# Second layer of a mixture of graph experts: an odd slot tile in a place of its own, pairs nested behind it, another order of the products, and a GpSimd drain after each expert

## The chip, the cores and the metric

The kernel runs on one core of a Trainium2 chip. The metric is the device time of one execution in microseconds. Before the change it is 805.65 us (median of 3 runs, 804.23 to 806.14).

## The reference, cut to what matters

A graph of 1250 nodes with rows of 512 features goes through a pre-norm attention layer and then through a mixture of four graph experts, of which each node keeps the two with the largest gates. Only the second part is touched:

```python
def sage_conv(h, W_l, b_l, W_r):
    aggr = segment_sum(h[src], dst) * inv_deg       # mean over the neighbours
    return aggr @ W_l + b_l + h @ W_r
...
gates = softmax(x @ gate_W + gate_b)
top_v, top_i = top_k(gates, 2)
...
for e in range(4):
    h = x
    for l in range(2):
        h = relu(sage_conv(h, Wl[e, l], bl[e, l], Wr[e, l]))
    # weighted by the gate where expert e is one of the node's two, and added to the output
```

The first layer of an expert is needed on all nodes, since the second averages over neighbours. The second is needed only on the nodes that chose the expert: 54, 917, 1049 and 480 nodes for experts 0 to 3 with these inputs.

## The kernel before, in words

**Layer 1.** For each expert, `layer1(t)` computes two tiles of 125 nodes at once. The 2x2 block product (own features and neighbour mean against Wr and Wl, each in column halves) is done with seven products P1 to P7 (four steps of a 128x256 fp32 matmul each, eight matmuls in the trace) where eight would be needed; sums of operands and results are VectorE's. The result is written to DRAM (`h1`, for gathering) and kept on chip as a high and a low half (`split`, L115 to L121: ScalarE writes h_hi, VectorE h_lo).

**Slots.** `number_slots` (L666) and `fill_slots` (L712) number the nodes of each expert: slot tile i (a "place") holds 128 of the chosen nodes, and `reads`, `writes` and `gate` hold for each slot the node's row and gate. An expert has NS = 10 places. The counts of nodes go into `many`, from which each engine loads them into a register.

**Layer 2.** For a place, GpSimd gathers with an indirect DMA the packed counts of its nodes' neighbours (`fetch_counts`, L787, tile asel, a ring of four), which `unpack` (L790) turns into a matrix AS: transposes on TensorE, digits on VectorE (L802), five casts and the copy of one column `inv` (L808) on ScalarE. It gathers the nodes' own rows of h1 (`fetch_own`, L813, tile hsel, a ring of two). `sums_of` multiplies AS with h_hi and h_lo of all ten node tiles (20 matmuls of 512 columns, p_s), `mean_of` scales with inv and transposes, `features` transposes the own rows with a ReLU. `pair_of_slots` (L944) then makes two places with the seven products, in the order P1, P7, P2, P4, P5, P6, P3; P1 and P7 lie in the halves of one PSUM bank. `one_of_slots` (L977) makes a single place with four products. `put` (L932) applies ReLU and gate on ScalarE (L935) and adds the tile into the output with an accumulating indirect DMA (L936); tile y is a ring of two.

**Control flow.** `second_layer` (L995) is a nest that calls itself: at place i, if the expert has more than (i+1) x 128 nodes the pair i, i+1 is made, and then, if there are more than (i+2) x 128 (L1011), the nest goes on at i+2; otherwise (the Else arm) place i is made alone. So a single place stands at the end of an expert. The outermost If (here `counts[e] > 0`) stands in the expert loop, L1017 to L1038.

**Order.** The tile scheduler orders the instructions of each engine within a block of the program; across the Ifs the order is that of the blocks. The first `layer1` call of the next expert is issued ahead of the Ifs of the current one, and its other calls, with the counts of its first four places, behind them. GpSimd issues all 82 indirect DMAs of a run in one queue. At the end `total` is loaded into a register and compared with the number of edges (L1374 to L1376); the branch jumps over a general version of the kernel that isn't needed here.

Of the kernel before, what the change touches and what calls it, by code (L numbers as in the profile page):

```python
# [42 lines left out]
def tile_sorted_graph(  # L43
# [92 lines left out]
        return t  # L136

    SLOTS = 128
    NS = -(-N // SLOTS)
    packs = dram.tile([N, SC + 1], F32, name="packs")  # L140


# [10 lines left out]
    sums = const.tile([T, ND * len(chunks)], F32, name="sums")  # L153
    ones_h = const.tile([128, 128], BF16, name="ones_h")
    nc.vector.memset(ones_h, 1.0)
    many = const.tile([1, NE], I32, name="many")
    AT = adj.tile([T, NT, N], F32R, name="AT")
    AT32 = AT.bitcast(F32)

# [492 lines left out]
    def bias_rows(e):  # L652
# [3 lines left out]

    first_bias = bias_rows(0)

    spots = xall[:, 3:8, :].rearrange("p a n -> p (a n)").bitcast(BF16).rearrange(
        "p (c n) -> p c n", n=SLOTS)  # L660
    tells = xall[:, 8:, :].rearrange("p a n -> p (a n)").bitcast(BF16)[:, :NE * NT * FLD * NS].rearrange(
        "p (c f q) -> p c f q", f=FLD, q=NS)

    book = ctx.enter_context(tc.tile_pool(name="book", bufs=1, side="right"))

    def number_slots():  # L666

        flat = chosen.rearrange("p e t -> p (e t)")  # L670
        p = bank("p_n")
        nc.tensor.matmul(p[:T, :NE * NT], before, flat, start=True, stop=True)
        nc.tensor.matmul(p[:T, NE * NT:2 * NE * NT], ones_h[:T, :T], flat, start=True, stop=True)
        pv = p[:T, :2 * NE * NT].rearrange("p (a e t) -> p a e t", a=2, e=NE)
        off = book.tile([T, NE, NT + 1], F32, name="off")
        nc.vector.memset(off[:, :, 0], 0.0)
        for t in range(NT):
            nc.vector.tensor_add(off[:, :, t + 1], off[:, :, t], pv[:, 1, :, t])
        nc.vector.tensor_copy(many, off[:1, :, NT])
        at = book.tile([T, NE, NT], F32, name="at")  # L680
        nc.vector.tensor_add(at, pv[:, 0], off[:, :, :NT])
        at = at.rearrange("p e t -> p (e t)")
        qt = book.tile([T, NE * NT], F32, name="qt")
        nc.vector.tensor_scalar(qt, at, 1.0 / SLOTS, -(0.5 - 0.25 / SLOTS), op0=OP.mult, op1=OP.add)
        nc.vector.tensor_scalar(qt, qt, ROUND, -ROUND, op0=OP.add, op1=OP.add)
        nc.vector.scalar_tensor_tensor(at, qt, float(-SLOTS), at, op0=OP.mult, op1=OP.add)

        nc.vector.scalar_tensor_tensor(qt, qt, 1.0, flat, op0=OP.add, op1=OP.mult)
        left = book.tile([T, NE, NT], F32, name="left")
        nc.vector.tensor_copy(left, g.rearrange("p t e -> p e t"))  # L690
        left = left.rearrange("p e t -> p (e t)")
        for f in range(2, FLD):
            nc.vector.tensor_copy(told[:, :, f], left)
            if f + 1 < FLD:
                nc.vector.tensor_sub(left, left, told[:, :, f])
        for e in range(NE):
            c = slice(e * NT, (e + 1) * NT)
            nc.vector.tensor_tensor(spots[:, c, :], steps_h[:, None, :].to_broadcast([T, NT, SLOTS]),
                                    at[:, c, None].to_broadcast([T, NT, SLOTS]), op=OP.is_equal)

        mine = mix_tiles[0][0].rearrange("p k n -> p (k n)").bitcast(BF16)[:T, :NE * NT * NS].rearrange(
            "p (c q) -> p c q", q=NS)
        nc.vector.tensor_tensor(mine, steps_h[:, None, 1:NS + 1].to_broadcast([T, NE * NT, NS]),
                                qt[:, :, None].to_broadcast([T, NE * NT, NS]), op=OP.is_equal)
        nc.vector.tensor_tensor(tells, mine[:, :, None, :].to_broadcast([T, NE * NT, FLD, NS]),
                                told[:, :, :, None].to_broadcast([T, NE * NT, FLD, NS]), op=OP.mult)
# [31 lines left out]
    while mean_whole:  # L738
        if len(mean_whole) == 1:
# [6 lines left out]
            first_mix = mix_weights(w0)  # L746
            mix_nodes(0)
        next_mean()
    counts = [nc.values_load(many[:1, e:e + 1], min_val=0, max_val=N,
                             skip_runtime_bounds_check_because="it is compared, and addresses nothing")  # L750
              for e in range(NE)]
    halves.release()
    node.release()
    adj.release()
# [172 lines left out]
    def mean_of(p, iv):  # L927
        agg = aggs()
        nc.vector.tensor_scalar(agg, p, iv, None, op0=OP.mult)  # L929
        return features(agg, gTs, AF.Copy)  # L930
# [8 lines left out]
    def halves_of(*names):  # L939
        for name in names:  # L940
            p = bank(name)
            yield from (p[:, h * HD:(h + 1) * HD] for h in range(2))

    def pair_of_slots(second, r, g, spare_sums, e, i):  # L944

        B11, B21, B22, T1, T2, T3, T4, bl1, br1 = second
        (A11, A21), (A12, A22) = r, g
        S1, S2, S3, S4 = (t.rearrange("p (k n) -> p k n", k=KF) for t in spare_sums)
        P1, P7, P2, P4, P5, P6 = halves_of("p_y", "p_y", "p_y")
        P3 = bank("p_y")[:, :HD]  # L950
        ya, yb = ys(), ys()
        C11, C12, C21, C22 = ya[:, :HD], ya[:, HD:], yb[:, :HD], yb[:, HD:]
        nc.vector.tensor_sub(S3, A11, A21)
        times(P1, (A11, B11))
        nc.vector.tensor_add(C11, P1, bl1)
        nc.vector.tensor_add(S1, A21, A22)
        times(P7, (S3, T3))
        nc.vector.tensor_sub(S2, S1, A11)
        nc.vector.tensor_add(C22, C11, P7)
        times(P2, (A12, B21))  # L960
        nc.vector.tensor_sub(S4, A12, S2)
        times(P4, (A22, T4))
        times(P5, (S1, T1))
        nc.vector.tensor_add(C12, P5, br1)
        times(P6, (S2, T2))
        nc.vector.tensor_add(C21, C22, P6)
        nc.vector.tensor_add(C22, C21, C12)
        nc.vector.tensor_add(C21, C21, P4)  # L968
        put(yb, e, i + 1)
        nc.vector.tensor_add(C12, C12, C11)  # L970
        nc.vector.tensor_add(C12, C12, P6)
        nc.vector.tensor_add(C11, C11, P2)
        times(P3, (S4, B22))
        nc.vector.tensor_add(C12, C12, P3)
        put(ya, e, i)

    def one_of_slots(second, r, p, iv, e, i):  # L977

# [13 lines left out]
        nc.vector.tensor_add(C12, C12, Q)  # L992
        put(y, e, i)

    def second_layer(of, e, i, own, AS, asel):  # L995

        (a, b), ivs, hs, h1 = *zip(*AS), of.hs, of.h1
        with tc.If(counts[e] > (i + 1) * SLOTS) as two:  # L998

            later = [fetch_counts(e * NS + n) for n in range(i + 4, min(i + 6, NS))]  # L1000
            p = [sums_of(a, hs), sums_of(b, hs)]
            g = [mean_of(p[0], ivs[0])]
            r = [features(v, rTs, AF.Relu) for v in own]
            if i + 2 < NS:
                own = [fetch_own(e * NS + n, h1) for n in (i + 2, i + 3)]
            if asel:
                AS = [unpack(v) for v in asel]
            g.append(mean_of(p[1], ivs[1]))
            pair_of_slots(of.second, r, g, of.spare_sums, e, i)
            if i + 2 < NS:  # L1010
                with tc.If(counts[e] > (i + 2) * SLOTS):  # L1011
                    second_layer(of, e, i + 2, own, AS, later)
        with two.Else():
            one_of_slots(of.second, own[0], sums_of(a, hs), ivs[0], e, i)

    ahead = [w0]
    now = Expert(0)  # L1017
    for e in range(NE):
        now.loads()
        for t in range(min(e, 1), NT // 2):  # L1020
            now.layer1(t)
            if t == NT // 2 - (2 if e == 0 else 3):
                asel = [fetch_counts(e * NS + i) for i in range(4)]
            if t == NT // 2 - (1 if e == 0 else 2):
                AS = [unpack(a) for a in asel[:2]]
        now.finish()
        own = [fetch_own(e * NS + i, now.h1) for i in range(2)]
        of = now
        if e + 1 == NE:
            of.mix_second()  # L1030
        else:
            now = Expert(e + 1)
            now.layer1(0)
            of.mix_second()
        of.spare_sums = [node_sums[(turns[0] + i) % 6] for i in range(2)] + \
            [vs.tiles[(vs.n + i) % 4] for i in range(2)]
        with tc.If(counts[e] > 0):  # L1037
            second_layer(of, e, 0, own, AS, asel[2:])  # L1038


@with_exitstack
# [325 lines left out]
@with_exitstack  # L1367
def tile_gat_then_moe_sage(ctx: ExitStack, tc: tile.TileContext, *args):
    nc = tc.nc
    flag = ctx.enter_context(tc.tile_pool(name="flag", bufs=1))  # L1370
    total = flag.tile([1, 1], I32, name="total")
    tile_sorted_graph(tc, *args, total)
    E = args[1].shape[0]
    counted = nc.values_load(total[:1, :1], min_val=0, max_val=1 << 24,  # L1374
                             skip_runtime_bounds_check_because="it is compared, and addresses nothing")
    with tc.If(counted != E):  # L1376
        tile_any_graph(tc, *args)

# [27 lines left out]
```

## Time and profile before

| | us |
|---|---|
| median of 3 runs | 805.65 (804.23 to 806.14) |
| profiled execution | 806.73 |
| its span | 805.0 |
| TensorE busy | 743.4 |
| VectorE busy | 505.8 |
| ScalarE busy | 265.8 |
| GpSimd busy | 147.4 |
| mean granted TensorE clock | 0.968 |

Layer 1 and layer 2 of the experts take the span from about 249 us to the end. A pair of places takes 24.0 us there, from start to start. The page counts matmuls, vector operations and issued DMAs as busy; branches, register loads and drains are not in its busy times but are in the trace. A timeline row gives start, duration, engine, line, operation, tiles, and in brackets the idle time of the engine before it with what ended it. A wait row gives the total, the number of times and the longest one. The gathers and puts of GpSimd are:

```profile
L813 POOL DMA_INDIRECT hsel<-h,reads x28 | 33.0, 1180 | 227.7 <-issue 94.9
L936 POOL DMA_INDIRECT out_dram<-y,writes x22 | 35.8, 1629 | 195.8 <-ACT y L935 155.6
...
L787 POOL DMA_INDIRECT asel<-packs,reads x32 | 35.4, 1106 | 66.7 <-DVE v L880 56.8
```

The numbers after the bar are the busy time, and the mean of one in ns; a row's DMA lands later than its instruction ends.

### The profile page before, as it was taken

How to read it: one execution, taken by the hardware profiler on the slowest of the kernel's cores; microseconds unless marked ns; L12 is line 12 of the kernel's file. 1: busy time of each engine (PE TensorE's matmuls, PEld its weight loads, DVE VectorE, ACT ScalarE, POOL GpSimd, SP SyncE). 2: the span in 40 equal slices, each digit the busy share in tenths (PEclk: the TensorE clock that was granted, in tenths of full speed). 3: DMA queues.
4: the chain of work that ended last, by engine and by line, in shares of the span. 5: the costliest groups of instructions: out<-in, count | busy, mean ns of one | idle time of the engine just before them, and what ended most of it. 6: DMA issues, size and time to landing. Idle time of an engine off the chain costs nothing. (4 is left out here: it accounts for less than half of the span.)

```text
span 805.0 us, 9845 instructions
## 1 busy us (share of the span) xinstructions
PE 743.4 (92%) x3448; PEld 597.0 (74%) x3448; DVE 505.8 (63%) x1152; ACT 265.8 (33%) x589; POOL 147.4 (18%) x125
## 2 busy tenths in 40 slices
PE   6899999999999999999999997999999997899960
PEld 4677545455998888788888886888888886788850
DVE  7987999599878569267743434678344343466340
ACT  5659766764300012112033322120333230132230
POOL 1000523222002001200313322103133212002220
PEclk9899999999999999999999999999999998999985
DMA  7000001010225412261303323612133224213131
GB/s 189 7 13 7 6 13 58 13 39 1 72 97 159 140 57 74 93 222 43 90 27 66 66 41 94 214 49 83 34 66 62 31 41 109 78 52 86 26 61 15
DMA packets 30331, 54.27 MB, mean 67 GB/s; under 512 B 5786, under 2 KB 8230, under 8 KB 30252
## 3 DMA queue, kind: packets, MB, share of 16 engines
q0 software_dynamic: 6944, 16.58, 10.2%
q1 hardware_dynamic: 15154, 20.80, 8.8%
q10 hardware_dynamic: 8154, 15.91, 5.8%
q8 instruction: 41, 0.67, 0.4%
q14 instruction: 38, 0.31, 0.1%
HBM read 34.10 MB, written 19.82 MB: 67 GB/s over the span
## 5 line engine op out<-in xcount | busy, mean ns | idle before, releaser
L431 PE MATMUL p_o<-hW,P 125*125 125x512 f32 x200 | 93.5, 609 | 2.3 <-DVE P L425 2.3
L923 PE MATMUL p_s<-h_hi,AS 125*128 125x512 f32 x220 | 89.0, 404 | 1.3 <-issue 1.3
L923 PE MATMUL p_s<-h_lo,AS 125*128 125x512 f32 x220 | 86.8, 394 | 0.0
L831 PE MATMUL p<-T,S 128*125 128x256 f32 x320 | 74.8, 386 | 3.1 <-DVE v L880 3.1
L118 ACT ACTIVATE h_hi<-v 125x512 fp32r<-125x512 f32 x40 | 25.2, 630 | 154.7 <-DVE v L895 132.9
L813 POOL DMA_INDIRECT hsel<-h,reads x28 | 33.0, 1180 | 227.7 <-issue 94.9
L936 POOL DMA_INDIRECT out_dram<-y,writes x22 | 35.8, 1629 | 195.8 <-ACT y L935 155.6
L831 PEld LDWEIGHTS p<-T,S 128*125 128x125 f32 x320 | 61.0, 191 | 13.1 <-DVE v L880 3.7
L929 DVE TENSOR_SCALAR agg<-p_s,inv 128x512 f32<-128x512 f32 x22 | 16.5, 751 | 79.8 <-PE p_f L821 43.4
L431 PEld LDWEIGHTS p_o<-hW,P 125*125 125x125 f32 x200 | 36.4, 193 | 39.4 <-issue 34.8
L806 ACT CAST AS<-digs 125x256 fp32r<-125x256 int32 x140 | 51.1, 403 | 19.4 <-DVE digs L802 12.3
L923 PEld LDWEIGHTS p_s<-h_hi,AS 125*128 125x128 f32 x220 | 41.5, 188 | 11.1 <-issue 1.7
L429 POOL TENSOR_TENSOR den<-den,P 125x375 f32<-125x375 f32 (+1 forms) x27 | 38.1, 1412 | 62.6 <-DVE P L425 59.4
L935 ACT ACTIVATE y<-y,gate 128x512 f32<-128x512 f32 x22 | 15.9, 723 | 99.7 <-DVE y L968 71.6
L923 PEld LDWEIGHTS p_s<-h_lo,AS 125*128 125x128 f32 x220 | 41.5, 189 | 9.4
L787 POOL DMA_INDIRECT asel<-packs,reads x32 | 35.4, 1106 | 66.7 <-DVE v L880 56.8
L823 ACT ACTIVATE gT<-p_f 128x512 f32<-128x512 f32 x22 | 13.1, 598 | 97.2 <-PE p_f L821 97.2
L378 DVE TENSOR_SCALAR first<-iota,low,val 125x250 bf16<-125x250 f16 x128 | 45.0, 413 | 0.3 <-PE p_a L382 0.3
L831 PE MATMUL p<-wr,h2T 128*125 128x256 f32 x160 | 39.6, 392 | 4.8 <-DVE S L645 4.1
L328 PE MATMUL p_h<-W_sb,hT 128*125 128x257 f32 x160 | 41.4, 417 | 2.2 <-ACT hT L185 2.1
L553 PE MATMUL p_ag<-AT,h_hi 125*128 125x416 f32 (+1 forms) x120 | 42.4, 355 | 0.0
L553 PE MATMUL p_ag<-AT,h_lo 125*128 125x416 f32 (+1 forms) x120 | 42.1, 352 | 0.0
(222 smaller groups left out, 1515.6 us busy)
## 6 DMA issues: line engine op xcount, KB each, us to landing
h<-v SPq DMA_DIRECT2D x40, 224.0 KB
wl<-in_L_gnn_Wl_dram ACTq DMA_DIRECT2D x7, 1024.0 KB
wr<-in_L_gnn_Wr_dram ACTq DMA_DIRECT2D x7, 1024.0 KB
out_dram<-x SPq DMA_DIRECT2D x10, 224.0 KB
x<-in_x_dram SPq DMA_DIRECT2D x1, 1120.0 KB
packs<-pack SPq DMA_DIRECT2D x10, 109.4 KB
h<-v SPq DMA_DIRECT2D x40, 26.0 KB
W_sb<-in_L_gnn_W_dram SPq DMA_DIRECT2D x4, 256.0 KB
```

Of the source, the lines that this page charges most:

```text
L118: nc.scalar.activation(hi, v, AF.Relu if relu else AF.Copy)
L328: nc.tensor.matmul(p[:T, :HD + 1], hT[:, k, :], W_sb[:, k, half, :], start=(k == 0), stop=(k == KF - 1))
L378: nc.vector.tensor_scalar(hs[:, :SC], iota[:EB, :SC], low[:, j:j + 1], val[:, j:j + 1], op0=OP.is_equal, op1=OP.mult)
L429: nc.gpsimd.tensor_add(den[:, :n], den[:, :n], P[:, :n])
L431: nc.tensor.matmul(po[i][:T, :], P[:, i * T:(i + 1) * T], hW[:, s - 1, :, :HD], start=(s == 1), stop=(s == NT))
L553: nc.tensor.matmul(p[:, :n], h2[s][i][:, m * 128:(m + 1) * 128], AT[:, s, c], start=(s == 0 and i == 0), stop=(s == NT - 1 and i == 1))
L787: nc.gpsimd.indirect_dma_start(a, None, packs, bass.IndirectOffsetOnAxis(reads[:, j:j + 1], 0))
L806: nc.scalar.copy(AS[:, d * SB:(d + 1) * SB, :], dig)
L813: nc.gpsimd.indirect_dma_start(r, None, h1, bass.IndirectOffsetOnAxis(reads[:, j:j + 1], 0))
L831: nc.tensor.matmul(p, A[:, k, :], B[:, k, :], start=(i == 0 and k == 0), stop=(i * KF + k == n - 1))
L923: nc.tensor.matmul(p, A[:, s, :], hs[s][f], start=(s == order[0] and f == 0), stop=(s == order[-1] and f == 1))
L936: nc.gpsimd.indirect_dma_start(out, bass.IndirectOffsetOnAxis(writes[:, j:j + 1], 0), y, None, bounds_check=N - 1, oob_is_err=False, compu ...
```

## The change

- NS becomes 11. Place 0 holds a tile of slots only if the expert's number of tiles is odd; otherwise it stays empty and the tiles lie in places 1 to 10. `number_slots` computes `odd` and shifts the places by it, and `many` gets a second row.
- `second_layer` goes. In the expert loop, `one_of_slots` makes place 0 under `If odds[e] > 0`, and then pairs 1-2, 3-4, 5-6, 7-8 and 9-10 follow in nested Ifs without Else. The counts of places 0 and 1 are unpacked and their own rows fetched ahead of the branches; place 2 is fetched and unpacked inside the first pair's If. So these steps are done for three more places in the run (experts 1 to 3).
- `pair_of_slots` makes P1, P2, P5, P6, P3, puts place i, and then makes P7 and P4 and puts place i+1. P1 and P6, P5 and P7, P2 and P4 share PSUM banks.
- GpSimd gets a `drain` behind each expert's Ifs. In the program as built it stands, for experts 0 to 2, ahead of the next expert's first `fetch_counts`; for expert 3 it stands at the end.
- `total` is loaded in the function that computes it and no longer in the caller; in the program as built, the load still stands behind the last expert.

```diff
@@ -136,7 +136,7 @@
         return t
 
     SLOTS = 128
-    NS = -(-N // SLOTS)
+    NS = -(-N // SLOTS) + 1
     packs = dram.tile([N, SC + 1], F32, name="packs")
 
 
@@ -153,7 +153,7 @@
     sums = const.tile([T, ND * len(chunks)], F32, name="sums")
     ones_h = const.tile([128, 128], BF16, name="ones_h")
     nc.vector.memset(ones_h, 1.0)
-    many = const.tile([1, NE], I32, name="many")
+    many = const.tile([1, 2, NE], I32, name="many")
     AT = adj.tile([T, NT, N], F32R, name="AT")
     AT32 = AT.bitcast(F32)
 
@@ -656,9 +656,9 @@
 
     first_bias = bias_rows(0)
 
-    spots = xall[:, 3:8, :].rearrange("p a n -> p (a n)").bitcast(BF16).rearrange(
+    spots = xall[:, 2:7, :].rearrange("p a n -> p (a n)").bitcast(BF16).rearrange(
         "p (c n) -> p c n", n=SLOTS)
-    tells = xall[:, 8:, :].rearrange("p a n -> p (a n)").bitcast(BF16)[:, :NE * NT * FLD * NS].rearrange(
+    tells = xall[:, 7:, :].rearrange("p a n -> p (a n)").bitcast(BF16)[:, :NE * NT * FLD * NS].rearrange(
         "p (c f q) -> p c f q", f=FLD, q=NS)
 
     book = ctx.enter_context(tc.tile_pool(name="book", bufs=1, side="right"))
@@ -676,7 +676,17 @@
         nc.vector.memset(off[:, :, 0], 0.0)
         for t in range(NT):
             nc.vector.tensor_add(off[:, :, t + 1], off[:, :, t], pv[:, 1, :, t])
-        nc.vector.tensor_copy(many, off[:1, :, NT])
+        nc.vector.tensor_copy(many[:, 0, :], off[:1, :, NT])
+
+        odd = book.tile([T, NE], F32, name="odd")
+        twos = book.tile([T, NE], F32, name="twos")
+        nc.vector.tensor_scalar(odd, off[:, :, NT], 1.0 / SLOTS, 0.5 - 0.25 / SLOTS, op0=OP.mult,
+                                op1=OP.add)
+        nc.vector.tensor_scalar(odd, odd, ROUND, -ROUND, op0=OP.add, op1=OP.add)
+        nc.vector.tensor_scalar(twos, odd, 0.5, -0.25, op0=OP.mult, op1=OP.add)
+        nc.vector.tensor_scalar(twos, twos, ROUND, -ROUND, op0=OP.add, op1=OP.add)
+        nc.vector.scalar_tensor_tensor(odd, twos, -2.0, odd, op0=OP.mult, op1=OP.add)
+        nc.vector.tensor_copy(many[:, 1, :], odd[:1, :])
         at = book.tile([T, NE, NT], F32, name="at")
         nc.vector.tensor_add(at, pv[:, 0], off[:, :, :NT])
         at = at.rearrange("p e t -> p (e t)")
@@ -685,7 +695,10 @@
         nc.vector.tensor_scalar(qt, qt, ROUND, -ROUND, op0=OP.add, op1=OP.add)
         nc.vector.scalar_tensor_tensor(at, qt, float(-SLOTS), at, op0=OP.mult, op1=OP.add)
 
-        nc.vector.scalar_tensor_tensor(qt, qt, 1.0, flat, op0=OP.add, op1=OP.mult)
+        by_expert = qt.rearrange("p (e t) -> p e t", e=NE)
+        nc.vector.tensor_tensor(by_expert, by_expert, odd[:, :, None].to_broadcast([T, NE, NT]),
+                                op=OP.subtract)
+        nc.vector.scalar_tensor_tensor(qt, qt, 2.0, flat, op0=OP.add, op1=OP.mult)
         left = book.tile([T, NE, NT], F32, name="left")
         nc.vector.tensor_copy(left, g.rearrange("p t e -> p e t"))
         left = left.rearrange("p e t -> p (e t)")
@@ -746,9 +759,12 @@
             first_mix = mix_weights(w0)
             mix_nodes(0)
         next_mean()
-    counts = [nc.values_load(many[:1, e:e + 1], min_val=0, max_val=N,
-                             skip_runtime_bounds_check_because="it is compared, and addresses nothing")
-              for e in range(NE)]
+    def loaded(v, most):
+        return nc.values_load(v, min_val=0, max_val=most,
+                              skip_runtime_bounds_check_because="it is compared, and addresses nothing")
+
+    counts, odds = ([loaded(many[:1, i, e:e + 1], N) for e in range(NE)] for i in range(2))
+    all_counted = loaded(total[:1, :1], 1 << 24)
     halves.release()
     node.release()
     adj.release()
@@ -946,33 +962,32 @@
         B11, B21, B22, T1, T2, T3, T4, bl1, br1 = second
         (A11, A21), (A12, A22) = r, g
         S1, S2, S3, S4 = (t.rearrange("p (k n) -> p k n", k=KF) for t in spare_sums)
-        P1, P7, P2, P4, P5, P6 = halves_of("p_y", "p_y", "p_y")
+        P1, P6, P5, P7, P2, P4 = halves_of("p_y", "p_y", "p_y")
         P3 = bank("p_y")[:, :HD]
         ya, yb = ys(), ys()
         C11, C12, C21, C22 = ya[:, :HD], ya[:, HD:], yb[:, :HD], yb[:, HD:]
         nc.vector.tensor_sub(S3, A11, A21)
         times(P1, (A11, B11))
-        nc.vector.tensor_add(C11, P1, bl1)
+        nc.vector.tensor_add(C21, P1, bl1)
         nc.vector.tensor_add(S1, A21, A22)
-        times(P7, (S3, T3))
         nc.vector.tensor_sub(S2, S1, A11)
-        nc.vector.tensor_add(C22, C11, P7)
+        nc.vector.tensor_sub(S4, A12, S2)
         times(P2, (A12, B21))
-        nc.vector.tensor_sub(S4, A12, S2)
-        times(P4, (A22, T4))
+        nc.vector.tensor_add(C11, C21, P2)
         times(P5, (S1, T1))
-        nc.vector.tensor_add(C12, P5, br1)
+        nc.vector.tensor_add(C22, P5, br1)
         times(P6, (S2, T2))
-        nc.vector.tensor_add(C21, C22, P6)
-        nc.vector.tensor_add(C22, C21, C12)
-        nc.vector.tensor_add(C21, C21, P4)
-        put(yb, e, i + 1)
-        nc.vector.tensor_add(C12, C12, C11)
-        nc.vector.tensor_add(C12, C12, P6)
-        nc.vector.tensor_add(C11, C11, P2)
+        nc.vector.tensor_add(C21, C21, P6)
+        nc.vector.tensor_add(C12, C21, C22)
         times(P3, (S4, B22))
         nc.vector.tensor_add(C12, C12, P3)
         put(ya, e, i)
+        times(P7, (S3, T3))
+        nc.vector.tensor_add(C21, C21, P7)
+        nc.vector.tensor_add(C22, C22, C21)
+        times(P4, (A22, T4))
+        nc.vector.tensor_add(C21, C21, P4)
+        put(yb, e, i + 1)
 
     def one_of_slots(second, r, p, iv, e, i):
 
@@ -992,27 +1007,6 @@
         nc.vector.tensor_add(C12, C12, Q)
         put(y, e, i)
 
-    def second_layer(of, e, i, own, AS, asel):
-
-        (a, b), ivs, hs, h1 = *zip(*AS), of.hs, of.h1
-        with tc.If(counts[e] > (i + 1) * SLOTS) as two:
-
-            later = [fetch_counts(e * NS + n) for n in range(i + 4, min(i + 6, NS))]
-            p = [sums_of(a, hs), sums_of(b, hs)]
-            g = [mean_of(p[0], ivs[0])]
-            r = [features(v, rTs, AF.Relu) for v in own]
-            if i + 2 < NS:
-                own = [fetch_own(e * NS + n, h1) for n in (i + 2, i + 3)]
-            if asel:
-                AS = [unpack(v) for v in asel]
-            g.append(mean_of(p[1], ivs[1]))
-            pair_of_slots(of.second, r, g, of.spare_sums, e, i)
-            if i + 2 < NS:
-                with tc.If(counts[e] > (i + 2) * SLOTS):
-                    second_layer(of, e, i + 2, own, AS, later)
-        with two.Else():
-            one_of_slots(of.second, own[0], sums_of(a, hs), ivs[0], e, i)
-
     ahead = [w0]
     now = Expert(0)
     for e in range(NE):
@@ -1022,7 +1016,7 @@
             if t == NT // 2 - (2 if e == 0 else 3):
                 asel = [fetch_counts(e * NS + i) for i in range(4)]
             if t == NT // 2 - (1 if e == 0 else 2):
-                AS = [unpack(a) for a in asel[:2]]
+                AS = [unpack(asel.pop(0)) for _ in range(2)]
         now.finish()
         own = [fetch_own(e * NS + i, now.h1) for i in range(2)]
         of = now
@@ -1034,8 +1028,32 @@
             of.mix_second()
         of.spare_sums = [node_sums[(turns[0] + i) % 6] for i in range(2)] + \
             [vs.tiles[(vs.n + i) % 4] for i in range(2)]
-        with tc.If(counts[e] > 0):
-            second_layer(of, e, 0, own, AS, asel[2:])
+        hs, h1, second = of.hs, of.h1, of.second
+        A, iv = AS.pop(0)
+        r = own.pop(0)
+        with tc.If(odds[e] > 0):
+            one_of_slots(second, r, sums_of(A, hs), iv, e, 0)
+        with ExitStack() as nest:
+            for i in range(1, NS, 2):
+                nest.enter_context(tc.If(counts[e] > i * SLOTS))
+                j = e * NS + i
+                if i == 1:
+                    own.append(fetch_own(j + 1, h1))
+                    AS.append(unpack(asel.pop(0)))
+
+                asel += [fetch_counts(e * NS + n) for n in range(i + 2 + len(asel), min(i + 6, NS))]
+                p = [sums_of(a, hs) for a, _ in AS]
+                ivs = [iv for _, iv in AS]
+                g = [mean_of(p[0], ivs[0])]
+                r = [features(v, rTs, AF.Relu) for v in own]
+                if i + 2 < NS:
+                    own = [fetch_own(j + 2 + n, h1) for n in range(2)]
+                    AS = [unpack(asel.pop(0)) for _ in range(2)]
+                g.append(mean_of(p[1], ivs[1]))
+                pair_of_slots(second, r, g, of.spare_sums, e, i)
+
+        tc.keep_in_program_order(nc.gpsimd.drain())
+    return all_counted
 
 
 @with_exitstack
@@ -1369,10 +1387,8 @@
     nc = tc.nc
     flag = ctx.enter_context(tc.tile_pool(name="flag", bufs=1))
     total = flag.tile([1, 1], I32, name="total")
-    tile_sorted_graph(tc, *args, total)
+    counted = tile_sorted_graph(tc, *args, total)
     E = args[1].shape[0]
-    counted = nc.values_load(total[:1, :1], min_val=0, max_val=1 << 24,
-                             skip_runtime_bounds_check_because="it is compared, and addresses nothing")
     with tc.If(counted != E):
         tile_any_graph(tc, *args)
```

## The prediction

> **What bounds the kernel now.** I read the page's busy times and slices first, then the PE timeline for its idle stretches, then the waits of the other engines that release PE there, and last the chain that ended last.
>
> ```profile
> span 805.0 us, 9845 instructions
> PE 743.4 (92%) x3448; PEld 597.0 (74%) x3448; DVE 505.8 (63%) x1152; ACT 265.8 (33%) x589; POOL 147.4 (18%) x125
> ...
> PE   6899999999999999999999997999999997899960
> ```
>
> TensorE is busy in 92% of the span, and its row of slices has dents only at the start, near 500 us (7), near 690 us (7, 8) and at the end (60). No product is removed by the change, so it can win only in dents, in small gaps inside the pairs, and behind the last product. The PE timeline has these (start, duration, line, tiles; the idle time before it and its releaser in brackets):
>
> ```profile
> 411.70 1.99 PE L831 MATMUL p_y<-wr,v 128*128 128x256 f32 x8 [0.17 <-DVE y L955]
> ...
> 497.28 3.23 PE L831 MATMUL p<-wr,h2T 128*125 128x256 f32 x7 [4.15 <-DVE S L645]
> ...
> 669.08 3.33 PE L831 MATMUL p_y<-wl,gT 128*128 128x256 f32 x7 [4.10 <-DVE y L987]
> ...
> 695.12 3.16 PE L831 MATMUL p<-T,S 128*125 128x256 f32 x7 [3.09 <-DVE v L880]
> ```
>
> The first sits in every one of the 10 pairs. At 497.28 expert 1 has ended; the named S is long done, and the trace has PE's own branch of L1011 taking 3.79 us there, a far jump over the else-arms. At 669.08 expert 2's ninth tile stands alone at the end. At 695.12 expert 3's layer 1 waits. Beside that, 7 products take 3.2 to 3.3 us after each gap of 3 us or more, against 7 x 0.216 + 0.16 = 1.7 us elsewhere: a long gap costs about 1.5 us more behind it. Two of these releasers stand on others:
>
> ```profile
> 668.51 0.42 DVE L987 TENSOR_TENSOR y<-p_y,b 128x256 f32<-128x256 f32 x1 [6.84 <-DMA out_dram<-y,writes]
> ...
> 687.19 0.19 ACT L808 COPY inv<-asel 128x1 f32<-128x1 f32 x1 [7.68 <-DMA asel<-packs,reads]
> 688.26 0.19 ACT L808 COPY inv<-asel 128x1 f32<-128x1 f32 x1 [0.88 <-DMA asel<-packs,reads]
> ```
>
> The lone tile needs the y buffer of the pair before it, whose put lands late; and ACT stands in a 1-column copy until the next expert's gathers land, with h_hi, and so DVE's h_lo (L121) and the next layer-1 product, behind it. The tail, by POOL's timeline:
>
> ```profile
> 779.91 1.62 POOL L936 DMA_INDIRECT out_dram<-y,writes  x1 [11.45 <-ACT y L935]
> 786.65 1.59 POOL L936 DMA_INDIRECT out_dram<-y,writes  x1 [5.12 <-DMA out_dram<-y,writes]
> ```
>
> PE's last product ends at 778.37. Two accumulating puts go one after the other, the second lands at 792.2, then POOL's semaphore increment (1.81), the load of `total` (0.31), the branch (2.5) and a POOL DRAIN of 6.76 us lead to 805.0. Other POOL drains in the trace took 0.19 (start of the run), 0.11 and 0.05 (right behind the long one). So a drain isn't long in itself; the long one stands behind all 82 indirect DMAs of the run, 0.082 us each.
>
> **The change part by part.** The sums p_s are 22: 1, 8, 9 and 4 tiles for experts 0 to 3. Experts 0 and 2 are odd.
>
> Gains. (1) Expert 1's exit: without else-arms the jump passes only over the body of i=9, and the jump over one pair's body took 0.34 us at 490.25. With PE's queue emptied, about 0.6 us is left: 4.15 - 0.6 and the 1.5 us of slow products, -5.0. (2) Expert 2's lone tile comes first, where both y buffers are free: 4.10 - 0.65, and 1.5, -5.0. (3) P1 and P7 no longer share a PSUM bank with a VectorE read between them: 10 x 0.18, -1.8. (4) Order in the pair: ya's put is issued about 2 us before the last product ends (P7 and P4, 3.46 us, lie behind P3), lands some 5.6 us later, and yb's put lands about 10.3 us after the last product, against 792.2 - 778.4 = 13.8: -3.5. (5) The last drain has 20 or so DMAs behind it instead of 82; at 0.082 each that is 1.65 for 6.76: -5.1. Sum of gains -20.4.
>
> Costs. (a) The even experts 1 and 3 skip the odd arm by a taken branch, for which PE waits out its own queue: 0.6 where the next layer's product lies ahead (expert 1), 1.3 in expert 3: +1.9. (b) Place 2 of each expert that reaches it is unpacked: 3 more unpacks of 4 transposes, 0.44 us on PE by the start times: +1.3. ACT's and DVE's part (5 casts, 5 digits) lies beside products. (c) number_slots gets 7 small VectorE operations of 0.16 to 0.18 us and an 11th column in L703 and L705 (2.80 us, a tenth). VectorE is without a gap from 231 to 248 us and PE waits for L705 at 242: +1.4. (d) In expert 3 nothing of a next layer covers the gathers. Own rows of places 0 and 1 are issued at 734.17 and 735.42, when h1 has landed. Place 2's own rows use a ring of two and follow the first landing (about 737.5), then come place 3's and 4's counts. The changed program has, on ACT, the copy of place 4's inv ahead of the fifth cast of place 2's AS; the second sum needs this cast. A gather lands 3.3 to 4.3 us after its start, so at 743 to 744.5, while PE wants it at about 739.5: 4.5, and 1.5 of slow products, +6.0. (e) The drains stand on POOL ahead of the next expert's first gathers (asel n=0, 1). Queued behind them are these gathers; ACT's inv copies wait for those, h_hi behind them, then h_lo, then PE. At 82 ns for 30 DMAs a drain takes about 2.5 us. Expert 2 to 3 had no slack (3.09 us gap): +2.5. At 1 to 2 and 0 to 1 h_lo stands behind more work in the changed order: +1.5 and +1.0. Sum +5.0. Expert 0 itself: about even, its far jump (3.33 us, a gap of 1.33 and one of 0.60) becomes a skip of the whole nest of some 1.8 on PE. (f) `total`: its load is written earlier, but in the changed program it still stands at the end: 0. Sum of costs 15.6.
>
> Of the drain the trace shows ends only. Low bound: 0.05 us at each place. High bound: 6.76 at each place, if the length isn't a matter of count. The Trainium skill ("VectorE: DVE Perf Modes", section The DRAIN you can't avoid) calls the drains that the runtime puts around a program constant, about 12 ns. SP's, ACT's, DVE's and PE's here took 7 to 13 ns and agree; POOL's 6.76 doesn't. By the rule (5) and (e) would both be near nothing: -15.3 + 10.6 = -4.7. By the row in proportion it is -20.4 + 15.6 = -4.8. I take the proportion, since the three short drains stand where few or no DMAs were issued. The second rule that speaks here is that of taken branches ("Runtime: NRT & Kernel Launch", section Instruction fetch mechanics): a target outside the two-page window must be fetched first[...]. By it each skip of an odd arm and each exit would cost a far jump, 3.3 to 3.8 us by the trace, in four places (skips in experts 1 and 3, exits of 1 and 2), about +11 against my sum. The row of 0.34 for a jump over a pair, longer than the odd arm, decides for the small price.
>
> Sum: 806.73 - 4.8 = 801.9 for the profiled execution, which lies 1.1 above the median of the runs, so 801 us.
>
> **The rivals.**
> A (the forecast): as summed, 797 to 805; chance 0.42.
> B: the same, but half of expert 3's stall (d) and of the late gathers (e) is hidden (the copy of inv, or the second sum, comes later than I read it): -20.4 + 15.6 - 5.5 = -10.3, 795 by the median, 793 to 797; chance 0.20. For it: of 7 waits of L808 for asel, 23.2 us in all, only one shows on PE.
> C (slower): each POOL drain costs about 6.8 us whatever was issued since the last. Then (5) is gone, and each drain delays the gathers by 4.3 us more than in (e), at three experts: -15.3 + 15.6 + 3 x 4 = +12, 808 to 820, near 817. With every drain at d, gains are 15.3 + 6.76 - d and costs 15.6 + 3 x (d - 2.5): level at d = 3.5 us, from where it decides. Chance 0.25, with other waits of the same size on POOL.
> D: the change doesn't do what it says at the end: the drain's length is set by something else in the last block, the last one stays near 6.8 and the earlier ones are short. -15.3 + 10.6 = -4.7, and up to 2 less if gathers still come later: 801 to 804, chance 0.13.
>
> **How the numbers follow.** A measurement of this kernel tells 0.3% (2.4 us) from no change. A is faster but for its upper end (0.32 of 0.42 faster, 0.07 level, 0.03 slower); B is faster; D 0.08 faster, 0.05 level; C 0.22 slower, 0.03 level. Faster 0.60, same 0.15, slower 0.25. The range goes from 793 (B's low end) to 814, within C, whose upper half is left out. Where it's faster, the likeliest range is 797 to 805.
>
> **What would show it.** (1) and (2): no PE gap above 1 us at expert 1's exit and at expert 2's single tile. (3): no 0.17 gap with releaser L955. (4): ya's put starts before the last product's end. (5): the last drain near 1.7 us and three others near 2.5. (d): one gap of 3 to 5 us in the second sum of expert 3. (e): the gap at expert 3's start 5 to 6 us. I'm wrong if the drains are near 7 us each, if the exits still show 3 us jumps, or if gathers come so late that layer 1 of experts 1 and 2 waits as well.

## The result, and the profile after

The changed kernel takes 799.77 us (median of 6 runs, 798.53 to 802.38) against 806.2 us before (6 runs): a ratio of 0.9924, 95% interval 0.9902 to 0.9945. The forecast was 801. The profiled execution took 799.66 us with a span of 797.9 us, 7.1 us less than the span before, at a mean granted clock of 0.974 instead of 0.968. The clock's rise comes of the shorter tail: behind the last product TensorE is idle and its clock 0.5, for 11 us of the span where it was 24.

The page of the changed kernel, its busy times and TensorE's slices:

```profile
PE 741.6 (93%) x3454; PEld 598.3 (75%) x3454; DVE 508.5 (64%) x1164; ACT 272.7 (34%) x610; POOL 149.8 (19%) x131
...
PE   6899999998998999999999999999999999698992
```

The dent near 500 us is gone, the one near 690 us is deeper (6), 8s are new near 190, 250 and 730 us, and the last slices are fuller. TensorE's timeline (start, duration, line, tiles, and the idle time before with its releaser) gives every gap above 0.9 us after 340 us:

```profile
496.57 1.99 PE L847 MATMUL p<-wr,h2T 128*125 128x256 f32 x8 [1.31 <-ACTq L1036]
...
517.39 1.99 PE L847 MATMUL p<-wr,S 128*125 128x256 f32 x8 [1.57 <-DVE v L898]
...
668.46 1.99 PE L847 MATMUL p<-wr,h2T 128*125 128x256 f32 x8 [1.31 <-ACTq L1036]
...
691.73 3.42 PE L847 MATMUL p<-T,S 128*125 128x256 f32 x8 [7.46 <-DVE v L896]
...
727.61 0.45 PE L811 MATMUL p_as<-ident,asel 128*125 128x128 f32 x2 [0.94 <-DVE v L913]
...
739.74 0.80 PE L939 MATMUL p_s<-h_hi,AS 125*128 125x512 f32 x1 [3.77 <-ACT AS L822]
```

The exits of experts 1 and 2 cost 1.31 us each where expert 1's cost 4.15, and no lone tile waits any more. New are a gap in expert 2's layer 1 (1.57), a larger one in expert 3's (7.46 for 3.09), the skip of the odd arm (0.94) and the stall in expert 3's second sum (3.77). Of a pair, the products are now gapless (its start-to-start time fell from 24.03 to 23.57 us):

```profile
414.01 1.89 PE L847 MATMUL p_y<-wl,gT 128*128 128x256 f32 x8
415.74 3.62 PE L847 MATMUL p_y<-wl,S 128*128 128x256 f32 x16
419.19 1.89 PE L847 MATMUL p_y<-wl,v 128*128 128x256 f32 x8
420.92 1.89 PE L847 MATMUL p_y<-wr,v 128*128 128x256 f32 x8
422.64 1.89 PE L847 MATMUL p_y<-wr,gT 128*128 128x256 f32 x8
```

The end, by GpSimd's timeline:

```profile
780.16 1.62 POOL L952 DMA_INDIRECT out_dram<-y,writes  x1 [8.72 <-ACT y L951]
786.28 1.57 POOL L952 DMA_INDIRECT out_dram<-y,writes  x1 [4.50 <-DMA out_dram<-y,writes]
```

TensorE's last product ends at 782.1, 3.7 us *later* than before (778.4). The first put starts 2 us ahead of that end, the second 4.2 us behind it (8.3 before), and the last drain takes 1.68 us instead of 6.76. So 26.6 us behind the last product became 15.8. In one line: the tail gave 10.8 us, the rest of the program lost 3.7.

### The profile page after: what moved, and what is told of

It reads as the page before. It is cut to its first block, busy times and chain, and to the rows that moved or that the text cites. A ratio compares the mean times of both kernels' runs of the same rounds, so it can differ in the third digit from the quotient of the medians.

```text
span 797.9 us, 9901 instructions
## 1 busy us (share of the span) xinstructions
PE 741.6 (93%) x3454; PEld 598.3 (75%) x3454; DVE 508.5 (64%) x1164; ACT 272.7 (34%) x610; POOL 149.8 (19%) x131
## 5 line engine op out<-in xcount | busy, mean ns | idle before, releaser
L829 POOL DMA_INDIRECT hsel<-h,reads x31 | 35.8, 1156 | 234.3 <-DMA h<-v 147.6
L822 ACT CAST AS<-digs 125x256 fp32r<-125x256 int32 x155 | 56.7, 403 | 22.7 <-DVE digs L818 17.3
L121 DVE SCALAR_TENSOR_TENSOR h_lo<-v,h_hi 125x512 fp32r<-125x512 f32 x40 | 27.4, 689 | 20.3 <-ACT h_hi L118 19.1
```

The source lines that it names most:

```text
L121: nc.vector.scalar_tensor_tensor(lo, v, 0.0, hi.bitcast(F32), op0=OP.max, op1=OP.subtract)
L822: nc.scalar.copy(AS[:, d * SB:(d + 1) * SB, :], dig)
L829: nc.gpsimd.indirect_dma_start(r, None, h1, bass.IndirectOffsetOnAxis(reads[:, j:j + 1], 0))
```

## The experiments

All times are medians, each against runs of the kernel before on the same chip (806.3 to 806.6); ratios have their 95% interval.

**Without the drains** (`no_drain`).

```diff
-        tc.keep_in_program_order(nc.gpsimd.drain())
```

> The changed kernel without the drains behind the experts; nothing else differs. Theory 1 (the drains hold up the next expert's gathers, and shorten the last drain in proportion to the DMAs since the one before): the PE gap at expert 3's start falls from 7.5 us to 3 or less, the one in expert 2's layer 1 (1.6 us) goes, and the last drain grows from 1.7 to about 7 us: PE gains 5 to 6, the tail loses 5, so 799 to 801 us, level with the changed kernel. Theory 2 (the gathers come late because the puts do, and the drain only spends time in which GpSimd waits anyway): the gaps stay, the last drain grows, 804 to 806. Theory 3 (the last drain's length doesn't depend on earlier drains): the last drain stays at 1.7 us and the kernel gets faster, 794.

798.48 us, 0.990 (0.986 to 0.994): level with the changed kernel. The gap at expert 3's start fell from 7.46 to 1.81, the one in expert 2's layer 1 went, TensorE ended at 772.1 instead of 782.1, and the last drain grew to 7.25 us. Theory 1 holds: the drains behind the experts cost about what they bring. GpSimd's timeline of the changed kernel behind expert 2 (the drain itself, 7.95 us from 671.79, has no row here):

```profile
670.80 1.58 POOL L952 DMA_INDIRECT out_dram<-y,writes  x1 [4.00 <-issue]
680.69 1.02 POOL L803 DMA_INDIRECT asel<-packs,reads  x1 [8.30 <-issue]
```

and without the drains:

```profile
669.16 1.58 POOL L952 DMA_INDIRECT out_dram<-y,writes  x1 [3.99 <-issue]
671.80 1.02 POOL L803 DMA_INDIRECT asel<-packs,reads  x1 [1.06 <-issue]
```

From put to first gather it is 9.9 us with the drain and 2.6 without. What waits for these gathers in the changed kernel is ScalarE:

```profile
684.44 0.19 ACT L824 COPY inv<-asel 128x1 f32<-128x1 f32 x1 [12.51 <-DMA asel<-packs,reads]
...
684.96 0.62 ACT L118 ACTIVATE h_hi<-v 125x512 fp32r<-125x512 f32 x1
```

A copy of one column holds ScalarE for 12.5 us (7.7 before); h_hi stands behind it, and then VectorE and the next product of layer 1.

**The drains behind the gathers** (`drain_behind`).

```diff
-                asel = [fetch_counts(e * NS + i) for i in range(4)]
+                asel = [fetch_counts(e * NS + i) for i in range(4)]; e and tc.keep_in_program_order(nc.gpsimd.drain())
...
-        tc.keep_in_program_order(nc.gpsimd.drain())
+    tc.keep_in_program_order(nc.gpsimd.drain())
```

> The changed kernel with the drain of experts 0 to 2 moved behind the next expert's first four gathers. Theory 1: the gathers are issued some 8 to 9 us earlier after experts 1 and 2, the gap at expert 3's start falls from 7.5 to 3 us or less and the 1.6 us gap in expert 2's layer 1 goes, while the last drain stays at 1.7 us: 793 to 795 us. Theory 2 (gathers late because of the puts): no change, 799 to 800. A drain there waits for the gathers in flight, some 4 to 5 us, with nothing queued behind it that is due: no price.

790.13 us, 0.981 (0.977 to 0.985), 9.6 less than the changed kernel. The drains took 7.5 to 10.9 us here (0.6 to 8.9 in the changed kernel), and no gap of TensorE comes of them: behind the last of the three, the next entry of GpSimd's queue, the own rows, starts 41 us after its end. The last one took 1.36 us. TensorE's gap at expert 3's start:

```profile
681.96 1.99 PE L847 MATMUL p<-T,S 128*125 128x256 f32 x8 [1.71 <-DVE v L896]
```

1.71 instead of 7.46, and eight matmuls in 1.99 us instead of 3.42. So it isn't a drain's length that counts here but what is queued behind it.

**Place 4's counts early** (`fourth_early`).

```diff
-        own = [fetch_own(e * NS + i, now.h1) for i in range(2)]
+        asel.append(fetch_counts(e * NS + 4)); own = [fetch_own(e * NS + i, now.h1) for i in range(2)]
```

> The changed kernel with the counts of place 4 gathered ahead of the own rows of places 0 and 1, instead of behind those of place 2; one more gather in the run. Theory 1 (the copy of place 4's inv ahead of the fifth cast holds up expert 3's second sum): the 3.8 us gap in the sum goes and the slow matmuls behind it too (20 of 0.43 instead of 0.23 would be 4, six are left: 1.2): 794 to 796 us. Rival (the fifth cast is late because of the own rows or of VectorE's digits): the gap stays at 3 us or more, 799 to 800.

796.25 us, 0.988 (0.984 to 0.991): 3.5 less than the changed kernel, with intervals that overlap slightly; in the traces TensorE ends 6.2 us earlier. ScalarE in the changed kernel, expert 3's first pair:

```profile
731.58 1.66 ACT L822 CAST AS<-digs 125x256 fp32r<-125x256 int32 x4 [2.14 <-DVE digs L818]
739.19 0.19 ACT L824 COPY inv<-asel 128x1 f32<-128x1 f32 x1 [5.94 <-DMA asel<-packs,reads]
739.28 0.40 ACT L822 CAST AS<-digs 125x256 fp32r<-125x256 int32 x1
```

and with the early gather:

```profile
730.99 0.19 ACT L824 COPY inv<-asel 128x1 f32<-128x1 f32 x1 [1.24 <-DVEq L1034]
731.87 1.96 ACT L822 CAST AS<-digs 125x256 fp32r<-125x256 int32 x5 [0.68 <-DVE digs L818]
```

Four casts, a wait of 5.94 us in a copy that the second sum doesn't need, and then the fifth cast that it needs; with the gather ahead, five casts in a row, and the 3.77 us gap is gone.

**The order of products alone** (`before_order`): the kernel before with the changed `pair_of_slots`, all else as before.

```diff
-        P1, P7, P2, P4, P5, P6 = halves_of("p_y", "p_y", "p_y")
+        P1, P6, P5, P7, P2, P4 = halves_of("p_y", "p_y", "p_y")
...
         times(P3, (S4, B22))
         nc.vector.tensor_add(C12, C12, P3)
         put(ya, e, i)
+        times(P7, (S3, T3))
...
+        put(yb, e, i + 1)
```

> The kernel before with only the new order of the products in a pair; Ifs, places and drain as before. Theory 1: the ten gaps of 0.17 us go (-1.8), ya's put starts before the last product ends and the second put lands 4 us earlier (-3.5 to -4.4), the last drain stays near 6.8: -5 to -6, 800 to 801 us by the median of before of 806. Rival (the order gains only in the tail, since the gaps come back at other products): -3.5 to -4.4, 802. Where expert 2's lone tile waits for the y buffer (6.8 us before), the yb put now comes last in its pair, but starts sooner than the ya put did: that gap of 4.1 us falls to 0 to 2, which would bring 2 to 3.5 more (797 to 799).

793.58 us, 0.985 (0.982 to 0.988). This is the surprise of the study: one part of the change, alone, gives twice what the whole gives. Its TensorE timeline at expert 2's lone tile, which stands last here as before, has no gap:

```profile
661.75 1.89 PE L831 MATMUL p_y<-wr,rT 128*128 128x256 f32 x8
663.48 1.03 PE L831 MATMUL p_y<-wl,rT 128*128 128x256 f32 x4
664.34 0.85 PE L831 MATMUL p_y<-wl,gT 128*128 128x256 f32 x3
```

The y buffer that the lone tile takes is the one whose put now starts ahead of the last product, so it is free in time. The 4.1 us that the prediction booked for the odd place come from the order already. The second put of its tail:

```profile
774.11 1.59 POOL L936 DMA_INDIRECT out_dram<-y,writes  x1 [4.88 <-DMA out_dram<-y,writes]
```

The last product ends at 769.6, the first put starts at 767.6, ahead of that end, the second one 4.5 us behind it, and the last drain still takes 6.76 us.

**Only the PSUM banks** (`before_banks`): the first pair of lines of that diff alone, the order of products as before.

> The kernel before with only the pairing of the products in PSUM banks changed (P1 with P6, P5 with P7, P2 with P4); the order in which products are made and tiles put stays. It splits the gain of the new order (12.8 us alone). Theory: the ten gaps of 0.17 us go, nothing else: -1.8, 804 to 805 against 806.3; the lone tile's gap of 4.1 us, the tail (second put 8.3 us behind the last product) and the last drain stay. Rival (the gaps come back at other products, or PE's clock takes the gain): within 0.5 us of before.

800.64 us, 0.993 (0.990 to 0.995): -6 where 1.8 was expected. A pair went from 24.03 to 23.57 us, as in the changed kernel, so the ten pairs gave 4.6, and the sharing of banks is their cause. The lone tile's gap stayed (3.13 us, 4.10 before). The single runs range from 794 us at a granted clock of 0.976 to 802 at 0.965 (for this see the last section); the remaining 1.4 us lie within that. So of the order's 12.8 us, 4 to 6 are the banks, and 7 to 9 the lone tile and the tail.

**The change with the old order** (`after_oldorder`): the changed kernel with the old `pair_of_slots`.

> The changed kernel with the old order of the products: odd places first, nest without Else, drains as changed. Theory (the order gives 1.8 in the pairs and 3.8 in the tail whatever the Ifs): 799.8 + 5.6 = 805 to 806 us, so that the rest of the change by itself is level with the kernel before (806). With the old order the lone tile is first, so its wait for the y buffer is gone in any case. Rival (the order matters more, since ya's put now also stands before the drain and the next gathers): 808 to 812, slower than before.

813.35 us, 1.0085 (1.0062 to 1.0109): slower than before. Without the order of products, the odd place, the nest and the drains together lose 7 us. Beside the pairs (10 x 0.46) and the tail (18.4 us behind the last product, 15.8 with the new order), the exits of experts 1 and 2 grew from 1.31 to 2.82 us: the row of the exit there reads

```profile
498.12 3.35 PE L847 MATMUL p<-wr,h2T 128*125 128x256 f32 x7 [2.82 <-ACTq L1037]
```

By the trace, TensorE's first product waits there until ScalarE has finished the pair's last `y`: that ended at 498.02, and the product started at 498.12. In the old order, four more VectorE operations stand ahead of this `y`. And seven matmuls took 3.35 us behind that gap, at a granted clock of 0.5.

**The numbering's price** (`order_numbers`): `before_order` with NS = 11 in the tiles of the numbering and the seven small operations, with the odd count multiplied by zero, so that the places and all else stay as before.

> The kernel before with the new order of products (793.6 us alone) and with the numbering's added work: seven small VectorE operations and NS = 11 in its tiles, but the odd count multiplied by zero, so that places, Ifs and second layer stay as before. Theory (VectorE is without a gap there): +1.5 to 3 us, 795 to 796.5, with the gap ahead of the slot product (L717) at 1.9 us instead of 0.8. Rival (the gaps of 1.9 and 1.4 us in the changed kernel come from another order of the instructions around it): within 0.5 us, 794.

796.26 us, 0.986 (0.983 to 0.990), against 793.58: +2.7, with intervals that overlap. The gap ahead of the slot product was 1.49 us instead of 0.79, and behind it the clock was at 0.5 for 3.4 us; from the numbering's first product to the first of layer 1 TensorE needed 23.7 us instead of 21.4. The size is as expected; the medians alone are only a weak proof of it.

**Drains without the new Ifs** (`order_drain`): `before_order` with a drain behind the next expert's gathers (as in `drain_behind`) and at the end.

> The kernel before with the new order of products (793.6 us alone) and with drains, put behind the next expert's first four gathers and at the end; the old Ifs and places. Theory 1 (the drain's gain is the last drain, 6.8 to 1.4 us, and it costs nothing where no due gather is queued behind it): 788 to 789 us. If this is level with the changed kernel that has both moves (786), the odd place and the nest are worth little; the old nest still pays 4.9 us at expert 1's exit, and the new one its numbers (2 to 3 us) and skips (1 to 2). Rival (a drain in this place holds the own rows of the next expert up): 792 to 796.

786.50 us, 0.976 (0.973 to 0.978), 7.1 less than `before_order`; last drain 1.20 us. So the drains' gain needs neither the odd place nor the new Ifs.

**Both moves in the changed kernel** (`both`): the diffs of `drain_behind` and `fourth_early`.

> The changed kernel with both of the moves that gained by themselves: drains behind the next expert's first four gathers (790.1 us alone against 799.8), and the counts of place 4 gathered ahead of the own rows (796.3 alone). They mend different gaps (7.5 us at expert 3's start, 3.8 us in its second sum), so their gains should add: 799.8 - 9.6 - 3.5 = 786 to 787 us. Rival: with the first gap gone, own rows and gathers of expert 3 come at another time and meet anyway, so the second gain is lost: 789 to 790.

784.47 us, 0.973 (0.970 to 0.976): the gains add, 15.3 us less than the changed kernel. It is the fastest version here. Against `order_drain` it is 2 us, within the intervals: whether the odd place and the nest are worth anything once the other parts stand rightly stays open.

**Without the bias wait** (`both_pinned`): `both`, with VectorE's subtraction of the second layer's biases kept where the program has it.

```diff
-            nc.vector.tensor_sub(br1, br1, bl1)
+            tc.keep_in_program_order(nc.vector.tensor_sub(br1, br1, bl1))
```

> The changed kernel with both moves (784.5 us), and with VectorE's subtraction of the second layer's biases (L929) kept where the program has it. In the changed kernel it stood ahead of L896 at 253 us, waiting for a bias load, and PE had a gap of 1.4 to 1.8 us behind it that the kernel before doesn't have. Theory: that gap goes, the rest of expert 0's layer 1 moves ahead of its Ifs: 782 to 783 us. Rival (layer 1 of expert 0 gives the time back at the next wait): 784 to 785.

785.91 us, 0.975 (0.972 to 0.977): no gain. The gap near 254 us fell only from 1.82 to 0.83, and a new one of 1.36 us stands at 401.6. The rival holds: the time is given back at other waits.

## Why the prediction was right, and where its parts were not

The time was right to 1.2 us, and the sign. But the sum came out right in part by luck: the prediction booked 5.3 us of gain for the order of products and a loss of 0.5 for all the rest, and alone they gave 12.8 and lost 7.0. Two errors of about 7 us offset each other.

| step | predicted | measured in the traces |
|---|---|---|
| (1) expert 1's exit | -5.0 | gap 4.15 to 1.31, eight matmuls 3.44 to 1.83: -4.4 |
| (2) expert 2's lone tile | -5.0 | gap 4.10 to an exit of 1.31, from 669.08 to the next layer 7.25 us, 4.39 for the same products at full clock (`before_banks`): -5.6 |
| (3) pairs | -1.8 | 24.03 to 23.57, ten times: -4.6 |
| (4) second put | -3.5 | start 8.3 to 4.2 behind the last product: -4.1 |
| (5) last drain | -5.1 | 6.76 to 1.68: -5.1 |
| (a) skips | +1.9 | 0.94 in expert 3, none above 0.3 in expert 1 |
| (b) three unpacks | +1.3 | not measured by itself; two transposes each, 62 in all for 56, so 0.7 by the same start times |
| (c) numbering | +1.4 | gap 0.70 to 1.86 and 3.4 us at half clock: 24.1 us instead of 21.3 to layer 1, +2.8; and a gap of 1.44 at a bias load |
| (d) fourth asel | +6.0 | gap 3.77, the next 22 matmuls 6.13 us instead of 3.59 (`fourth_early`): +6.3 |
| (e) late gathers | +5.0 | 1.57, and 7.46 for 3.09: +5.9 |

The tail gave 1.6 us more than (4) and (5) together; 1.2 of them are a semaphore increment of GpSimd's (1.81 to 0.57), which no step named.

(1), (5) and (d) were right in mechanism and near in size, and so was the place of the wait in (e). The exit of 1.31 instead of 0.6 has a cause that the step didn't name: the wait for ScalarE's last `y`, which in the changed kernel ran from 495.75 to 496.47, TensorE's product starting at 496.57; that the one waits for the other is read from the trace and from the longer exits of `after_oldorder`, and no run takes it away.

(b) counted four transposes for an unpack; the rows have two. (3) was mis-sized by more than a factor of two. The step took the idle time of the row at 411.70, 0.17 us. But a row's idle time is counted from the modelled end of the matmul before it. By the starts, the seventh product should begin at 410.07 + 6 x 0.216 = 411.37 and began at 411.70, and the next part lost another 0.1: 0.43 us a pair, close to the 0.46 from 24.03 to 23.57.

(2) was right as a sum and wrong as an attribution: it said that the lone tile's wait goes because the tile comes first. `before_order` shows it gone with the tile still last. In the sum the gain was to be had once; as a judgement on the odd place it was false.

(e) had the right place and the wrong law. The step gave a drain 0.082 us for each DMA since the last one, 2.5 us in the middle of the run. The law holds where all DMAs have landed: 7 of them took 0.63 us, 14 took 1.20, 16 took 1.36, 20 took 1.68, 82 took 6.76 and 88 took 7.25. Behind an expert the last put is still in flight, and there the drains took 8.85 and 7.95 us: the put issued at 499.01 landed at 507.55 and the drain ended at 508.82; that of 670.80 landed at 678.43, and the drain ended at 679.74. In all seven traces with such drains, the 14 behind experts 1 and 2 ended 1.2 to 1.3 us after the last landing, ahead of the gathers or behind them. So such a drain ends only when what was in flight has landed. By the prediction's own sign (drains near 7 us each) this step was wrong for two of the four, and the +5.0 for the measured +5.9 is near by chance: its 2.5, 1.5 and 1.0 us for experts 2 to 3, 1 to 2 and 0 to 1 became 4.4, 1.6 and none. It is rival C's price of a drain, though not its reason; the loss was less than C's +12, since expert 1 to 2 had slack of some 6 us by an estimate (the gathers came 7.3 us later by the rows of expert 2, and 1.57 us of gap came of it), the drain behind expert 0 took 0.63 us, and the last drain did fall. Rival D (the last drain stays long) is refuted by 1.68, B (the fetches and the stall half hidden) by the gaps of 7.46 and 3.77.

The rule of the Trainium skill that was weighed there ("VectorE: DVE Perf Modes", section The DRAIN you can't avoid: constant, some 12 ns) doesn't fit GpSimd's drains in any run here (the other engines' took 7 to 17 ns before and after); the row, in proportion, was the right choice for the last drain, and too small for the others. That of taken branches ("Runtime: NRT & Kernel Launch", section Instruction fetch mechanics) speaks of far targets, and was rightly not applied to short jumps. At expert 1's exit TensorE's branch took 3.79 us before and 0.17 after, and still 4.51 in `before_order`, with a gap of 4.87; the skip of an odd arm shows a gap of 0.94 at most. The jump over expert 0's whole nest took 3.82, beside products that were queued before it. Far jumps were dear and near ones cheap, in line with the section; what is fetched in the far ones, no trace here shows.

What the prediction didn't see is that one part carried the gain: +7.0 us without the order, -12.8 by the order alone, -6.4 together. Nor is its 1.5 us for the slow products behind a long gap a constant; the last section has what decides it.

## What to carry to other kernels

Before a drain or any blocking instruction is put on a queue, look at the next entry of that queue and when it is due: here the drains between experts cost 10 us of TensorE's time ahead of four gathers and nothing to be seen behind them. Where a result is stored in two accumulating puts, order the products so that the first put starts under the last products; here this also freed its buffer and shortened the exits. And take a gap's cost from start-to-start times over several tiles, not from one row's idle time.

## What the runs showed that was not expected

Behind a TensorE gap of 2.8 us or more, eight matmuls took 3.15 to 3.6 us in most cases instead of 1.8 (behind 4.15, 7.46 and 4.8), but not in all: gaps of 3.69, 3.13 and 2.81 us in `before_banks`' profiled execution cost nothing behind them, as did 2.93 in `order_drain`. The traces have what decides it. The clock that TensorE is granted is 1 or 0.5 in them, and it changes only on a grid of 3.41 us. Two neighbouring stretches of that grid (start and end, length, busy time of each engine, and behind them PEclk, the granted clock, with DMA share and GB/s) at expert 1's exit in the kernel before, with its gap of 4.15 us:

```profile
493.97:497.38 3.41, 0.10 (x1) 0.14 (x2) 2.45 (x6) 1.15 (x2) 1.62 (x1) 1.00 0.12 13
497.38:500.79 3.41, 3.41 (x9) 2.68 (x10) 0.00 (x0) 0.00 (x0) 1.19 (x1) 0.50 0.83 229
```

and in `before_banks`, with its gap of 3.69 us:

```profile
491.71:495.12 3.41, 1.43 (x7) 0.92 (x5) 2.91 (x8) 1.44 (x2) 1.30 (x1) 1.00 0.03 7
495.12:498.53 3.41, 1.70 (x8) 1.53 (x9) 0.88 (x2) 0.00 (x0) 0.32 (x2) 1.00 0.48 115
```

The first gap left TensorE (the first busy time) 0.10 us of work in one stretch, and the next stretch ran at 0.5: matmuls started every 0.427 us instead of 0.216. The second gap lay across two stretches with 1.43 and 1.70 us of work, and the clock stayed at 1. So it is after 250 us in all twelve traces: each of the 29 full-clock stretches in which TensorE was busy for at most 37% was followed by one at 0.5, and none of the 1793 with 41% or more. From 0.5 it came back behind stretches with 85% or more, and not behind those with up to 82%, so that the gap of 4.10 us ahead of the lone tile cost two stretches and not one. (Ahead of 250 us, with shorter products, the border is less sharp: some stretches with 45% to 58% were followed by 0.5 too.) The grid lies elsewhere against the start of each trace. So whether a gap of some 3 to 4 us costs its own length alone, or up to 1.7 us more for each stretch at 0.5, depends on where it falls in that execution; by their mean clock this is the likely reason why the runs of `before_banks` lie between 794 and 802 us, though only one of them has a trace.
